# A graph layer on one core: one gather in nine blocks becomes 128 single-row transfers from SyncE

## The chip, the cores and the metric

The kernel runs on one core of a Trainium2 chip. The metric is the device time of one launch in microseconds (us); a version is compared by its median over several launches. [...]

## The reference

8192 nodes with 256 channels, 131072 edges with 64 attributes. `src` is random, `dst` is sorted. All float32.

```python
msg = relu(x[src] + edge_attr @ w_e + b_e)
agg = segment_sum(msg, dst, 8192)
h_local = bn1(relu((x + agg) @ w1 + b1) @ w2 + b2 + x)
# attention inside groups of 32 nodes, 4 heads of 64
q, k, v = split(x @ in_w.T + in_b)
h_attn = bn2(attention(q, k, v) @ out_w.T + out_b + x)
o = h_local + h_attn
o = bn3(o + relu(o @ m_w1 + m_b1) @ m_w2 + m_b2)
return layernorm(x + o)
```

`bn` is a scale and an offset for each channel.

## The kernel before

**Edges.** They are cut into 128 blocks of 1024, in the order of `dst`. A block passes through these steps:

- `gather` (L160): eight indirect DMAs on POOL, each of which fetches 128 rows of 1 KB by an index list into one eighth of the buffer `xs`. There are four `xs` buffers, so block b+4 can be fetched once block b's messages are made. The first 20 blocks fetch from `x`; later ones from `xb`, a copy of `x` in DRAM to which `b_e` has been added.
- `load_edges` (L176): four SP transfers of 128 KB bring the edge attributes into `ea` (two buffers, loaded two blocks ahead of use).
- `edge_transpose` (L193, DVE) turns them, `edge_products` multiplies by `w_e` on PE (L211) into the PSUM bank `pe`, one of two, a bank for each half (pair) of the block. For the first 20 blocks it also puts `b_e` there (L206).
- `edge_messages`: DVE adds `pe` and `xs` (L234, one instruction for each pair), ACT applies relu (L238).
- `edge_hot` (L246) compares indices to make 0/1 matrices; `edge_sums` adds messages by destination on PE (L255, sixteen matmuls a block), ACT copies the result to `ws` (L275); `edge_place` puts it into the right node columns on PE (L290), and DVE adds it to `xT` (L299).

**Nodes.** They are taken in 16 chunks of 512 (eight blocks). `load_nodes` (L306) brings a chunk's 512 KB into `xn` (four buffers) from SP, `attention_front` transposes it on PE (L444, ACT copies it to `xT` at L445) and multiplies by `in_w` (L455), `attention_back` does scores, softmax and the rest, and `dense` runs the two MLPs (matmuls L558), the layer norm, and an SP store of 512 KB from `y` (L616). The last chunk is done by `dense_rows`, 128 nodes at a time: it writes `x` plus the constant row `c3row` into `y` (L630), `sum_of_x` brings that into PSUM as the first term of the output, the layers follow (L641 and on), the norm writes `y` a second time, and SP stores it (L685).

**The copy `xb`.** In the first fourteen blocks or so, `copy_load` (L702) brings 512 KB or 1 MB of `x` into `xp`, `copy_stream` adds `b_e` on DVE (L708) and SP stores it to `xb` (L710). `xp` lies in buffers that `dense` uses later.

**Order.** PE runs in the order of the program text, and until block 26 DVE and ACT do so too; the other engines' instructions, SP's among them, are put in order by a scheduler. The node work is written as generators in four streams, and `work.run(us)` takes steps from them worth that much estimated PE time. A step that yields `REST` sets its stream aside for two calls of `run`:

```python
        if "xn" not in st:
            load_nodes(n0, st, pool)
            yield REST
```

Up to block 104 (`TAIL`) the main loop takes two blocks a turn: gathers for two blocks ahead; products, messages and next loads of the first and of the second block, sums of the turn before; and node work in portions of 0.3, 0.2 and 0.5 of the turn's allowance (0.2, 0.1, 0.2, 0.5 after block 26). After block 104 a planner goes block by block, with estimated due times. `came` is the time at which a block's last gather is expected:

```python
        came = [7.9 + 10.035 * (i + 1) for i in range(NB)]
```

From block 122 (`SPLIT`) on, it takes a block's two pairs one by one. In the very last block the messages are made group by group (256 edges; five additions, the last group in two halves), all issued at one place; then fourteen of the sixteen sums (all but the last gather's), a step of the last `dense_rows`, and the remaining sums.

**What a gather fetches.** Gather t of a block takes edges 128 t to 128 t + 127 of it; within these, edge e lands on partition 32 (e mod 4) + e div 4.

Of the kernel before, what the change touches and what calls it, by code (L numbers as in the profile page):

```python
# [9 lines left out]
FP = mybir.dt.float32  # L10
I32 = mybir.dt.int32
AF = mybir.ActivationFunctionType
ALU = mybir.AluOpType
AX = mybir.AxisListType
PSUM = bass.MemoryType.PSUM
DRAM = bass.MemoryType.DRAM
PE = mybir.EngineType.PE

P = 128
# [4 lines left out]
NB = E // BE  # L24
NH = 4
# [21 lines left out]
LN_EPS = 1e-5  # L47
REST = -1.0
PAUSE = -2.0

# [23 lines left out]
def gnn_kernel(ctx: ExitStack, tc: tile.TileContext, x, src, dst, edge_attr, w, out):  # L74
# [31 lines left out]

    srci = const.tile([P, NB, TB], I32, name="srci")
    rel = const.tile([P, NB, TB], FP, name="rel")
    wrow = const.tile([P, NB], FP, name="wrow")
    width = const.tile([1, 1], I32, name="width")  # L110
# [41 lines left out]

    xs_of = {}

    def gather(b):
        xs = epool.tile([P, NH, TJ, C], FP, name="xs", tag="xs", bufs=4)
        for h in range(NH):
            for j in range(TJ):
                idx = srcd[:, b * NH + h, j : j + 1] if b < ND else srci[:, b, h * TJ + j : h * TJ + j + 1]
                nc.gpsimd.indirect_dma_start(  # L160
                    out=xs[:, h, j, :],
                    out_offset=None,
                    in_=x if b < NX else xb[:, :],
                    in_offset=bass.IndirectOffsetOnAxis(ap=idx, axis=0),
                )
        xs_of[b] = xs
# [48 lines left out]

    def next_edges(b):
        if b < NB:
            edge_transpose(b)
        if b + 2 < NB:
            load_edges(b + 2)  # L220

    def edge_messages(b, pairs=range(0, NH, 2)):

        xs = xs_of[b]
        if b not in msg_of:
            msg_of[b] = epool.tile([P, NH, TJ, C], FP, name="msg", tag="msg", bufs=3)
        msg = msg_of[b]
        n = 2 if b < NB - 1 else 1
        for h in pairs:
            pe = pe_of.pop((b, h))  # L230
            for u in range(0, 2, n):
                hs = slice(h + u, h + u + n)
                for js in [slice(0, TJ)] if n == 2 or h + u < NH - 1 else [slice(j, j + 1) for j in range(TJ)]:
                    nc.vector.tensor_add(  # L234
                        msg[:, hs, js].rearrange("p u i c -> p i u c"), pe[:, js, u : u + n, :],
                        xs[:, hs, js].rearrange("p u i c -> p i u c"),
                    )
                    nc.scalar.activation(msg[:, hs, js], msg[:, hs, js], AF.Relu)  # L238
        between()
# [68 lines left out]
    with tc.tile_pool(name="setup", bufs=1) as sp:  # L308
# [125 lines left out]
    def attention_front(n0, st, pool, bank):  # L434
        if "xn" not in st:
            load_nodes(n0, st, pool)
            yield REST
        xn = st["xn"]
        xT = st["xT"] = pool.tile([P, KC, CH], FP, name="xT", tag="xT", bufs=4)
        hA = st["hA"] = pool.tile([P, KC, CH], FP, name="hA", tag="hA", bufs=4)  # L440
        for k in range(KC):
            ps = bank()
            for t in range(TN):
                nc.tensor.transpose(ps[:, t * P : (t + 1) * P], xn[:, t, k * P : (k + 1) * P], ident)  # L444
            nc.scalar.copy(xT[:, k, :], ps)  # L445
            nc.scalar.activation(
                hA[:, k, :], xT[:, k, :], AF.Identity, scale=s12[:, k : k + 1], bias=cA[:, k : k + 1]
            )
        yield 0.9

        qk = st["qk"] = pool.tile([P, 2 * KC, CH], FP, name="qk", tag="qk")
        for o in range(2 * KC):
            ps = bank()
            for k in range(KC):
                nc.tensor.matmul(  # L455
                    ps, inT[:, k, o * P : (o + 1) * P], xT[:, k, :], start=(k == 0), stop=(k == KC - 1)
                )
# [86 lines left out]

    def dense(n0, st, pool, bank, a=0, z=CH, own=("h1", "m1", "zT", "y", "")):

# [57 lines left out]
        for wt, ts in groups:  # L604
            nc.scalar.activation(rstd[:wt, ts], mv[:wt, ts, 1], AF.Sqrt, bias=eps_t[:wt])
        st["dense"] = z == CH
        yield 0.9 * part
# [6 lines left out]
        for wt, ts in groups:  # L614
            n = wt * (ts.stop - ts.start)
            nc.sync.dma_start(  # L616
                out[ds(n0 + a + ts.start * P, n), :].rearrange("(t p) c -> p t c", p=wt), y[:wt, ts, :]
            )
        yield 0.0

    def dense_rows(n0, st, pool, bank, a, own=("h1", "m1", "zT", "y", ""), ahead=False):
# [82 lines left out]
    def copy_stream(i):  # L704
        for _, c, n in steps[i] if 0 <= i < len(steps) else []:
            xp = xp_of[c]
            for r in range(n * TN):
                nc.vector.tensor_add(xp[:, r, :], xp[:, r, :], be)  # L708
                if r == n * TN - 1:
                    nc.sync.dma_start(rows(xb, c, n), xp)  # L710
                    xp_of.pop(c)
                yield
# [73 lines left out]
    placed = -1  # L786
    with tc.manual_schedule(engines={PE}):

# [8 lines left out]
        for c in range(NCH):  # L797
            st, before, same = chunk[c], chunk[c - 1], chunk[c - 4]
            front = attention_front(c * CH, st, npool, bank)
            if c < 2:  # L800
                next(front)
            work.add(
# [43 lines left out]
        while b < TAIL:  # L846
# [60 lines left out]
        def onward(at):  # L907
            at[:] = [at[0] + 1, 0] if at[1] or at[0] < SPLIT else [at[0], 1]

        while l < NB:  # L910
# [11 lines left out]
            elif p[0] < NB and (p[0] - 1, p[1]) < tuple(m):  # L922
                times[2] = half.get((p[0] - 1, p[1]), added[p[0] - 1])
            if tuple(m) < tuple(p):
                times[3] = came[m[0]]
                if m[0] >= SPLIT and not m[1]:
                    times[3] -= 2.5
            if t >= times[0]:
# [20 lines left out]
            elif t >= times[3]:  # L949

                with ExitStack() as behind:
                    for i, ins in newest.items():
                        if m[0] >= SPLIT or i in ("ws", "xT"):
                            behind.enter_context(tc.issue_after(ins))
                    edge_messages(m[0], (2 * m[1],) if m[0] >= SPLIT else range(0, NH, 2))
                if m[0] < SPLIT:
# [4 lines left out]
            elif t >= times[2]:  # L961
                i, k = p
                if not k and i + 2 < NB:
                    gather(i + 2)
                edge_products(i, (2 * k,) if i >= SPLIT else range(0, NH, 2))
                if k or i < SPLIT:
                    next_edges(i + 2)
                if not k:
                    edge_hot(i)
# [4 lines left out]
        work.finish()  # L974
    fast.close()

# [122 lines left out]
```

## Time and profile before

| | |
|---|---|
| runs | 1317.26, 1316.10, 1314.17 us, median 1316.1 |
| profiled execution: its own time / its span | 1317.09 / 1315.3 us |
| mean granted PE clock in it | 0.968 |
| busy: PE, DVE, POOL, ACT | 91%, 61%, 74%, 45% of the span |
| DMA: bytes, mean rate | 240.34 MB, 183 GB/s |
| chain that ended last: PE, POOL, issue, DVE, DMA | 33%, 32%, 15%, 9%, 7% |
| gathers: 144 from `x`, 864 from `xb` | 969 and 949 ns busy each |
| `ea` loads / `xn` loads / stores of `y` | 512 of 128 KB / 16 of 512 KB / 14 of 512 KB |
| `xp` loads and `xb` stores | 10 of 512 KB and 3 of 1 MB of each |

The span runs from the first to the last instruction; the time of the launch includes what lies around it. Busy shares are averages over stages with different limits: in the first 200 us the DMA engines also carry weights and the copy `xb`. "issue" in the chain is time in which an engine waited for nothing that the profile shows. The first 16 gathers take their indices from a buffer of their own and are listed apart from the 144 and the 864.

### The profile page before, as it was taken

The numbers are of one execution on the slowest core, as the hardware profiler recorded it, in microseconds if no ns is written. First come the engines' busy times: TensorE is split into PE (matmuls) and PEld (weight loads), VectorE is DVE, ScalarE is ACT, GpSimd is POOL, SyncE is SP. The second block draws the span as 40 slices with busy tenths as digits, with TensorE's granted clock in tenths as the row PEclk, the third lists the DMA queues.
The fourth block names the chain that finished last, engine by engine and source line by source line (L and its number), as shares of the span: only waits on it lengthen the run. The fifth ranks groups of instructions, "written<-read, shape, count | busy, mean of one in ns | idle before, by whom it ended". The sixth has DMA issues, their size and how long they took to land.

```text
span 1315.3 us, 21031 instructions
## 1 busy us (share of the span) xinstructions
PE 1200.4 (91%) x7671; PEld 722.5 (55%) x7671; DVE 799.3 (61%) x1630; ACT 587.3 (45%) x842; POOL 977.2 (74%) x1032
## 2 busy tenths in 40 slices
PE   5987989999999989898997998889898999989897
PEld 3544655556555555554554554545555555555665
DVE  6567665756666565745746574565647558475653
ACT  2524343454546263443545444354454445453432
POOL 7777777777777777777777777777777777777772
PEclk8988999999999989998999999989899999999998
DMA  9999876677766666665767666666667567656741
GB/s 241 302 311 271 266 205 174 173 183 195 176 171 173 171 176 164 184 162 154 190 165 184 157 183 169 153 184 171 170 168 191 148 170 190 165 165 159 194 133 50
DMA packets 148921, 240.34 MB, mean 183 GB/s; under 512 B 27950, under 2 KB 112204, under 8 KB 148044
## 3 DMA queue, kind: packets, MB, share of 16 engines
q0 software_dynamic: 49152, 134.28, 38.6%
q1 hardware_dynamic: 98572, 104.65, 29.3%
q8 instruction: 62, 1.02, 0.3%
q14 instruction: 47, 0.39, 0.1%
q10 hardware_dynamic: 1088, 0.00, 0.0%
HBM read 222.06 MB, written 16.78 MB: 182 GB/s over the span
## 4 chain that ended last, share of the span: by engine, by line
PE 33%; POOL 32%; issue 15%; DVE 9%; DMA 7%; ACT 4%; SPq 0%; DVEq 0%; POOLq 0%; ACTq 0%
POOL xs L160 32%; PE at L558 8%; PE pe L211 7%; DMA xs<-xb,srci 4%; PE at L455 4%; PE pw L255 3%; DVE msg L234 3%; PE l L290 2%; PE at L469 2%; PE at L536 2%; PE pe L206 1%; DMA xs<-in_x_dram,srci 1%; DVE bd L516 1%; ACT pr L496 1%; PE at L524 1%
## 5 line engine op out<-in xcount | busy, mean ns | idle before, releaser
L160 POOL DMA_INDIRECT xs<-xb,srci x864 | 820.3, 949 | 263.2 <-issue 251.0
L238 ACT ACTIVATE msg<-msg 128x1024 f32<-128x1024 f32 (+1 forms) x259 | 269.9, 1047 | 407.1 <-DVE msg L234 401.6
L234 DVE TENSOR_TENSOR msg<-pe,xs 128x1024 f32<-128x1024 f32 (+1 forms) x259 | 306.5, 1206 | 203.8 <-PE pe L211 81.1
L211 PE MATMUL pe<-we,eaT 64*128 64x256 f32 x2048 | 268.2, 397 | 16.4 <-ACT pr L496 10.2
L211 PEld LDWEIGHTS pe<-we,eaT 64*128 64x128 f32 x2048 | 192.9, 191 | 121.4 <-issue 63.0
L160 POOL DMA_INDIRECT xs<-in_x_dram,srci x144 | 139.6, 969 | 43.9 <-issue 40.8
L255 PE MATMUL pw<-msg,oh 128*32 128x256 f32 x2048 | 130.0, 383 | 1.1 <-ACT msg L238 0.8
L455 PE MATMUL at<-xT,inT 128*128 128x512 f32 x256 | 121.2, 599 | 3.2 <-ACT xT L445 3.2
L558 PE MATMUL at<-hA,mw 128*128 128x512 f32 (+1 forms) x256 | 116.3, 580 | 2.8 <-DVE hA L568 2.5
L558 PE MATMUL at<-m,mw 128*128 128x512 f32 (+1 forms) x256 | 111.4, 579 | 0.0
L193 DVE STREAM_TRANSPOSE eaT<-ea 128x512 f32<-128x512 f32 x128 | 90.0, 703 | 21.1 <-PE pe L211 19.2
L255 PEld LDWEIGHTS pw<-msg,oh 128*32 128x32 f32 x2048 | 60.0, 109 | 63.3 <-issue 21.4
L290 PEld LDWEIGHTS l<-oh,ws 128*128 128x128 f32 x512 | 72.4, 192 | 26.2 <-issue 20.3
L290 PE MATMUL l<-oh,ws 128*128 128x160 f32 (+4 forms) x512 | 84.2, 304 | 1.7 <-ACT ws L275 1.6
L455 PEld LDWEIGHTS at<-xT,inT 128*128 128x128 f32 x256 | 46.6, 190 | 57.0 <-issue 46.9
L458 ACT ACTIVATE qk<-at,vec 128x512 f32<-128x512 f32 x64 | 43.8, 684 | 70.6 <-PE at L455 70.5
L558 PEld LDWEIGHTS at<-m,mw 128*128 128x128 f32 x256 | 48.1, 193 | 48.4 <-issue 45.4
L558 PEld LDWEIGHTS at<-hA,mw 128*128 128x128 f32 x256 | 46.8, 192 | 50.6 <-issue 41.1
L246 DVE TENSOR_TENSOR oh<-iota_n,rel 128x128 f32<-128x128 f32 x256 | 57.5, 278 | 20.8 <-PE pw L255 20.7
L558 PE MATMUL at<-xT,w 128*128 128x512 f32 (+1 forms) x128 | 61.2, 615 | 6.8 <-DVE xT L299 6.8
L558 PE MATMUL at<-h,w 128*128 128x512 f32 (+1 forms) x128 | 59.8, 590 | 8.2 <-ACT oT L531 6.0
L574 ACT ACTIVATE m<-at,vec 128x512 f32<-128x512 f32 (+1 forms) x64 | 42.1, 658 | 53.8 <-PE at L558 53.7
(153 smaller groups left out, 1250.5 us busy)
## 6 DMA issues: line engine op xcount, KB each, us to landing
ea<-in_edge_attr_dram SPq DMA_DIRECT2D x512, 128.0 KB
xs<-xb,srci POOLq DMA_INDIRECT x864
xn<-in_x_dram SPq DMA_DIRECT2D x16, 512.0 KB
out_dram<-y SPq DMA_DIRECT2D x14, 512.0 KB
xp<-in_x_dram SPq DMA_DIRECT2D x10, 512.0 KB
xb<-xp SPq DMA_DIRECT2D x10, 512.0 KB
xp<-in_x_dram SPq DMA_DIRECT2D x3, 1024.0 KB
xb<-xp SPq DMA_DIRECT2D x3, 1024.0 KB
```

Of the source, the lines that this page charges most:

```text
L160: nc.gpsimd.indirect_dma_start(out=xs[:, h, j, :], out_offset=None, in_=x if b < NX else xb[:, :], in_offset=bass.IndirectOffsetOnAxis(ap= ...
L193: nc.vector.transpose(eaT, ea[:, QR:].rearrange("p (g d) -> p g d", d=ED)[:, :, :QR])
L211: nc.tensor.matmul(pe[:, i, u, :], eaT[rows, h + u], we[rows, :], start=(b >= NX), stop=True, skip_group_check=True)
L234: nc.vector.tensor_add(msg[:, hs, js].rearrange("p u i c -> p i u c"), pe[:, js, u : u + n, :], xs[:, hs, js].rearrange("p u i c -> p i u c"),
L238: nc.scalar.activation(msg[:, hs, js], msg[:, hs, js], AF.Relu)
L246: nc.vector.tensor_tensor(oh[:, ts], iota_n[:, None, :WN].to_broadcast([P, TB // 2, WN]), rel[:, b, ts, None].to_broadcast([P, TB // 2, WN ...
L255: nc.tensor.matmul(pw[h * WN : (h + 1) * WN, i, :], oh_of[b][:, h * TJ + j, :], msg_of[b][:, h, j, :], start=(j == 0), stop=(j == TJ - 1), ...
L290: nc.tensor.matmul(l2[:, k, at : at + wn], ws[:, i, k * P : (k + 1) * P], oh2[:, i, :wn], start=(i == 0 and k == 0), stop=(i == last), ski ...
L455: nc.tensor.matmul(ps, inT[:, k, o * P : (o + 1) * P], xT[:, k, :], start=(k == 0), stop=(k == KC - 1))
L458: nc.scalar.activation(qk[:, o, :], ps, AF.Identity, bias=v_("in_b", o))
L558: nc.tensor.matmul(ps, wt[:, k, o * P : (o + 1) * P], act[:, k, :], start=(k == 0), stop=(k == nk - 1))
L574: newest["relu"] = nc.scalar.activation(m1[:, o, :], layer(mw1, KC, o, hA), AF.Relu, bias=v_("m_b1", o)).ins
```

## The change

In nine blocks, 17, 31, 44, 57, 70, 83, 96, 109 and 122, the eighth gather is left out. Its 128 rows are fetched by 128 transfers of 1 KB that SP starts, each with its address in a register; a `TENSOR_LOAD` on SP fills 16 registers at a time from `srcs`, the clamped indices times 1024. The rows land in `xr` (two buffers). `fetch_rows` spreads them: four rows at each of five places in a turn of two blocks, ten a block in the planner. In such a block the second pair's addition is split in three, the last of which takes `xr` for `xs`.

SP now runs in the order of the text, like PE. So that its transfers are not issued before their data are ready, `put_off` keeps some of them (`ea` loads of the main loop, the `xb` stores, the stores of `y`) for a later `catch_up`. `dense` also asks for the `xn` of the chunk four ahead after it is done with its own. The node work's last portion of 0.5 is cut into 0.3 and 0.2, with rows between: the streams at `REST` see one more `run` a turn.

`dense_rows` writes `x` plus the constant into `xc`, a buffer apart from `y`. The last block's messages are issued group by group, each with a due time. `came` counts the gathers that there are, 1.2544 us each.

```diff
+ROW = 4 * C
+RT = NH * TJ - 1
+ROW_BLOCKS = (17, *range(31, NB, 13))
+RB, RL = 10, 16
...
+    def row_stream():
+        for b in ROW_BLOCKS:
+            while len(xr_of) > 1 or not (b < NX or copied[0]):
+                yield 0
+            xr = xr_of[b] = epool.tile([P, C], FP, name="xr", tag="xr", bufs=2)
+            for e0 in range(0, P, RL):
+                _, rows = nc.values_load_multi_w_load_instructions(
+                    srcs[b : b + 1, e0 : e0 + RL], engines=[SP], min_val=0, max_val=(N - 1) * ROW,
...
+                for i, row in enumerate(rows):
+                    p = (e0 + i) % EQ * QR + (e0 + i) // EQ
+                    nc.sync.dma_start(xr[p : p + 1, :].bitcast(U8), flat[b >= NX][ds(row, ROW)].unsqueeze(0))
...
+                    yield 1
+    row_by_row = row_stream()
+    def fetch_rows(n):
+        for _ in range(n):
+            next(row_by_row, None)
 def gather(b):
...
+                if b in ROW_BLOCKS and h * TJ + j == RT:
+                    continue
...
+    def put_off(turns, do):
+        later.append([turns, do])
+    def catch_up(n=1):
+        for entry in list(later):
+            entry[0] -= n
+            if entry[0] <= 0:
+                later.remove(entry)
+                entry[1]()
...
+    def next_edges(b, turns=0):
         if b < NB:
             edge_transpose(b)
         if b + 2 < NB:
-            load_edges(b + 2)
+            if turns:
+                put_off(turns, lambda: load_edges(b + 2))
+            else:
+                load_edges(b + 2)
...
 def edge_messages(b, pairs=range(0, NH, 2), of_pair=range(2)):
...
+                last = b in ROW_BLOCKS and h + u + n == NH
+                if last:
...
+                    xr = xr_of.pop(b)
+                    nc.vector.tensor_add(msg[:, hs, 0, :], pe[:, 0, u : u + n, :], xs[:, hs, 0, :])
+                    for v in range(u, u + n - 1):
+                        nc.vector.tensor_add(msg[:, h + v, 1, :], pe[:, 1, v, :], xs[:, h + v, 1, :])
+                    nc.vector.tensor_add(msg[:, NH - 1, 1, :], pe[:, 1, u + n - 1, :], xr)
...
+        nc.vector.tensor_scalar(srcs, srci_r[:, RT * P : (RT + 1) * P], 0.0, float(N - 1), ALU.max, ALU.min)
+        nc.vector.tensor_scalar(srcs, srcs, float(ROW), None, ALU.mult)
...
 def dense(n0, st, pool, bank, a=0, z=CH, own=("h1", "m1", "zT", "y", ""), turns=0):
+        catch_up(1000)
...
+        if turns and n0 // CH + 4 < NCH:
...
+            put_off(2, load_ahead)
...
+        if turns:
+            put_off(turns, store)
+        else:
+            store()
...
 def dense_rows(n0, st, pool, bank, a, own=("h1", "m1", "zT", "y", ""), ahead=False):
-        nc.vector.tensor_add(y, st["xn"][:, a // P, :], c3row)
+        xc = pool.tile([P, C], FP, name="xc", tag=own[2])
+        nc.vector.tensor_add(xc, st["xn"][:, a // P, :], c3row)
...
-            nc.tensor.matmul(ps, ident, y, start=True, stop=False, skip_group_check=True)
+            nc.tensor.matmul(ps, ident, xc, start=True, stop=False, skip_group_check=True)
...
-                    nc.sync.dma_start(rows(xb, c, n), xp)
-                    xp_of.pop(c)
+                    put_off(1, lambda c=c, n=n: nc.sync.dma_start(rows(xb, c, n), xp_of.pop(c)))
...
-    with tc.manual_schedule(engines={PE}):
+    with tc.manual_schedule(engines={PE, SP}):
...
-                work.add(DENSE, summed(c), dense(c * CH, st, npool, bank))
+                work.add(DENSE, summed(c), dense(c * CH, st, npool, bank, turns=4))
...
-                next_edges(b + 2)
+                next_edges(b + 2, 1)
+            fetch_rows(2 * RB // 5)
...
-            next_edges(b + 3)
+            next_edges(b + 3, 2 if b else 1)
+            fetch_rows(2 * RB // 5)
...
             work.run((0.3 if stated[0] else 0.1) * per)
+            catch_up()
+            fetch_rows(2 * RB // 5)
             copy_load(b // 2)
+            copied[0] = b > 2 * len(steps)
...
             work.run(0.2 * per)
+            catch_up()
+            fetch_rows(2 * RB // 5)
...
-            work.run(0.5 * per)
+            work.run(0.3 * per)
+            fetch_rows(2 * RB // 5)
+            work.run(0.2 * per)
...
-        came = [7.9 + 10.035 * (i + 1) for i in range(NB)]
+        came = [7.9 + 1.2544 * (TB * (i + 1) - sum(r <= i for r in ROW_BLOCKS)) for i in range(NB)]
...
+                if m[0] == NB - 1:
+                    times[3] -= 2.5 * (NH - 1 - m[1])
+                elif m[0] >= SPLIT and not m[1]:
+                    times[3] -= 5.0
...
+                    if m[0] == NB - 1:
+                        edge_messages(m[0], (m[1] // 2 * 2,), [m[1] % 2])
```

More of the change, by code (lines that the diff above doesn't have):

```diff
@@ L17 @@
 PE = mybir.EngineType.PE
+SP = mybir.EngineType.SP
+ACT = mybir.EngineType.Activation
 P = 128
@@ L150, in bank2 @@
         return pps.tile([P, 2, CH], FP, name="pe", tag="pe", bufs=2)
-    xs_of = {}
+    xs_of, xr_of, xr_full = {}, {}, set()
+    flat = [a.bitcast(U8).rearrange("n c -> (n c)") for a in (x, xb[:, :])]
+    copied = [False]
+    def row_stream():
[6 more added lines that the diff above has]
+                    srcs[b : b + 1, e0 : e0 + RL], engines=[SP], min_val=0, max_val=(N - 1) * ROW,
+                    skip_runtime_bounds_check_because="the indices are clamped to the rows of x when they are kept",
+                )
+                for i, row in enumerate(rows):
+                    p = (e0 + i) % EQ * QR + (e0 + i) // EQ
+                    nc.sync.dma_start(xr[p : p + 1, :].bitcast(U8), flat[b >= NX][ds(row, ROW)].unsqueeze(0))
+                    if e0 + i == P - 1:
+                        xr_full.add(b)
+                    yield 1
[3 more added lines that the diff above has]
+            next(row_by_row, None)
     def gather(b):
@@ L543, in attention_back, with dense @@
             yield 1.7
-    def dense(n0, st, pool, bank, a=0, z=CH, own=("h1", "m1", "zT", "y", "")):
+    def dense(n0, st, pool, bank, a=0, z=CH, own=("h1", "m1", "zT", "y", ""), turns=0):
         assert st["done"]
@@ L606, in dense, with load_ahead @@
         st["dense"] = z == CH
+        if turns and n0 // CH + 4 < NCH:
+            c = n0 // CH + 4
+            def load_ahead():
+                if "xn" not in chunk[c]:
+                    load_nodes(c * CH, chunk[c], pool)
+            put_off(2, load_ahead)
         yield 0.9 * part
@@ L613, in dense, with store @@
             )
[L614 to L618, printed above, removed]
+        def store():
+            for wt, ts in groups:
+                n = wt * (ts.stop - ts.start)
+                nc.sync.dma_start(
+                    out[ds(n0 + a + ts.start * P, n), :].rearrange("(t p) c -> p t c", p=wt), y[:wt, ts, :]
+                )
+        if turns:
+            put_off(turns, store)
+        else:
+            store()
         yield 0.0
@@ L907, in onward @@
         def onward(at):
-            at[:] = [at[0] + 1, 0] if at[1] or at[0] < SPLIT else [at[0], 1]
+            last = 0 if at[0] < SPLIT else NH - 1 if at is m and at[0] == NB - 1 else 1
+            at[:] = [at[0] + 1, 0] if at[1] == last else [at[0], at[1] + 1]
         while l < NB:
```

37 lines of the change are left out of this document (23 added, 14 removed).

## The prediction

> **What bounds the kernel now.** I read the page first: engine times, the forty slices, the costliest groups.
>
> ```profile
> span 1315.3 us, 21031 instructions
> ...
> PE 1200.4 (91%) x7671; PEld 722.5 (55%) x7671; DVE 799.3 (61%) x1630; ACT 587.3 (45%) x842; POOL 977.2 (74%) x1032
> ...
> POOL 7777777777777777777777777777777777777772
> ...
> DMA  9999876677766666665767666666667567656741
> ...
> L160 POOL DMA_INDIRECT xs<-xb,srci x864 | 820.3, 949 | 263.2 <-issue 251.0
> ...
> L160 POOL DMA_INDIRECT xs<-in_x_dram,srci x144 | 139.6, 969 | 43.9 <-issue 40.8
> ```
>
> PE has the largest share, but POOL's row of slices is the telling one: 7 everywhere, never a dip, until the last. Its 26% of idle time is cut evenly between the gathers and belongs to "issue". Two more views say that POOL waits for nobody: its waits, and the gather's own line with its first and last start.
>
> ```profile
> POOL xs L160 <- issue: 298.8, 973, 2.7
> ...
> POOL xs L160 <- DVE msg L234: 2.4, 8, 0.3
> ```
> ```profile
> L160 POOL DMA_INDIRECT xs<-xb,srci x864: 942/946/1087, 209.0 to 1291.2; - x173
> ```
>
> No wait on DVE is longer than the 0.3 us that every gather shows anyway, so no gather waited for its buffer. 864 gathers start between 209.0 and 1291.2: 1082.2/863 = 1.254 us each. The kernel is a row of 1024 gathers at 1.254 us, with a start before it and a tail after it. For it to stay so when POOL gets less to do, PE must have room; the stretches tell:
>
> ```profile
> 60.00:105.00 45.00, 38.65 (x275) 24.36 (x273) 28.58 (x59) 15.10 (x22) 34.34 (x36) 0.92 1.04 314
> 105.00:130.00 25.00, 17.54 (x101) 9.55 (x100) 18.68 (x43) 10.58 (x16) 18.91 (x21) 0.86 0.98 276
> ...
> 350.00:850.00 500.00, 461.75 (x2900) 271.22 (x2896) 295.63 (x577) 227.88 (x310) 378.43 (x400) 0.98 0.66 172
> 850.00:1050.00 200.00, 181.47 (x1108) 108.22 (x1108) 119.17 (x239) 95.69 (x132) 151.57 (x160) 0.92 0.63 171
> 1050.00:1292.00 242.00, 226.13 (x1505) 139.81 (x1504) 151.71 (x317) 106.59 (x167) 183.21 (x194) 1.00 0.63 165
> ```
>
> First number after the stretch is PE's busy time. It idles 38 us of 500, 19 of 200, 16 of 242. The last columns are DMA share and GB/s: full before 130 us, two thirds later.
>
> **The gathers removed.** In blocks 17, 31, 44 ... 122 the eighth gather goes: nine blocks, 9 x 1.254 = 11.3 us off POOL. In the changed order of instructions POOL has 16 + 143 + 856 = 1015 gathers. All of it lies on the path as long as no gather starts to wait. PE must then do the same work in 1.25 us less per thirteen blocks (about 130 us); its idle time by the rows above is 8 to 12 us per 130. So I count the full 11.3.
>
> A rule speaks against this. The Trainium skill, "DMA: Bandwidth & Descriptors", section "Issuing engines are not separate DMA queues": transfers started by different engines share the same 16 engines, and spreading the starts only saves the sequencer's starting time, "which is usually small relative to the DMA itself". By it moving rows to SyncE gives about nothing. The trace differs here: with the DMA share at 0.66 the starting time itself, 1.254 us, is the limit.
>
> **What SyncE gets.** 9 x 128 = 1152 one-row transfers, and a register load per 16 rows.
>
> ```profile
> L176 SPq DMA_DIRECT2D ea<-in_edge_attr_dram x512: 311/432/1795, 3.2 to 1251.9; - x171
> ```
> ```profile
> L326 SPq DMA_DIRECT2D vec_r<-in_L_gnn_bn_g_dram x3: 231/233/268, 11.2 to 16.1; - x3
> ```
> ```profile
> L978 SPq TENSOR_LOAD <-width x1: 533/533/533, 1312.0 to 1312.0; - x1
> ```
> ```profile
> 0.75 2.05 DMA srcd<-in_src_dram
> ...
> 9.71 5.54 DMA dsti_r<-in_dst_dram
> ...
> 16.76 5.34 DMA in_r<-in_L_gnn_in_w_dram
> ```
>
> No one-row transfer with its address in a register is in this trace. From below it costs SyncE 0.233 us (vec_r), from above 0.432 (ea); I take 0.35. Ten rows a block: 3.5 us, the register load 0.5, four ea loads 1.7: about 6 of the 10 us that a block takes. In the changed order every transfer waits for the eighth before it, so landing times count too: 2.05 us for a small one on a quiet queue, 5.3 to 5.5 for half a megabyte and more in a busy one. Fourteen transfers per block at a mean of 3 us are 14 x 3 / 8 = 5.3 us. Later than 200 us SyncE thus keeps up, and the rows cost nothing; their cover is that slack of some 4 us per block.
>
> **Before 200 us it is not covered.** SyncE is now kept in program order, and the DMA engines are full. From the first load of block 2 to the last of block 17 the changed queue holds 223 transfers, 128 of them rows; before it held 93.
>
> ```profile
> 49.37 1.75 SPq L176 DMA_DIRECT2D ea<-in_edge_attr_dram  x4
> ...
> 84.68 0.38 SPq L306 DMA_DIRECT2D xn<-in_x_dram  x1
> ...
> 105.84 0.34 SPq L710 DMA_DIRECT2D xb<-xp  x1
> ```
> ```profile
> 104.01 1.15 PE L290 MATMUL l<-oh,ws 128*128 128x112 f32 x8
> 105.08 1.13 PE L206 MATMUL pe<-be,sel 64*128 64x512 f32 x4
> 106.05 1.03 PE L211 MATMUL pe<-we,eaT 64*128 64x256 f32 x8
> ...
> 121.97 1.09 PE L444 MATMUL at<-ident,xn 128*128 128x128 f32 x8
> 124.94 1.13 PE L455 MATMUL at<-xT,inT 128*128 128x512 f32 x2 [1.87 <-ACT xT L445]
> 126.25 4.56 PE L455 MATMUL at<-xT,inT 128*128 128x512 f32 x10 [0.19 <-ACT xT L445]
> ```
> ```profile
> 67.94 0.70 DVE L193 STREAM_TRANSPOSE eaT<-ea 128x512 f32<-128x512 f32 x1
> ...
> 114.79 2.35 DVE L234 TENSOR_TENSOR msg<-pe,xs 128x1024 f32<-128x1024 f32 x2
> ...
> 186.00 1.23 DVE L234 TENSOR_TENSOR msg<-pe,xs 128x1024 f32<-128x1024 f32 x1 [0.50 <-PE pe L211]
> ```
> ```profile
> 127.18 0.95 POOL L160 DMA_INDIRECT xs<-in_x_dram,srci  x1 [0.30 <-DVE xp L708]
> ...
> 188.84 0.94 POOL L160 DMA_INDIRECT xs<-in_x_dram,srci  x1 [0.30 <-DVE oh L279]
> ```
>
> One wait stands out. Chunk 2's node load went out at 84.68 and its transposes ran at 121.97. Splitting the last stretch of attention work in two makes a rest of two turns shorter, so PE reaches these transposes right after the placement that stood at 104.01, ahead of block 8's products. Their load now follows, on SyncE, the store that left at 105.84, four rows and two loads. It leaves at about 109; with 2.5 MB in front and itself, at 314 GB/s, it lands 8 us later, some 117 (from below: 109 + 5.3 = 114; from above 124, with the rows' own landings in the chain). PE stands still from about 105 to 117; queued behind are block 8's products, and DVE waits for those. Transposes 1.1, the wait for ACT 1.9, eight matmuls 3.6 (4.56 for ten), a first pair of products 1.1 + 1.0: first message at 125.5, second 1.7 later and 1.2 long, done by 128.5 to 130 instead of 117.1. The gather of block 12, which takes block 8's buffer, wants to start at 127.2. So POOL waits 2 to 3 us. Against that, PE's 7.5 idle us in 105 to 130 are used up by the same wait, and the tightest later buffer (block 14's messages end at 187.2, the gather starts at 188.84: 1.6 us) gains what POOL has already lost. I count +3.0 us, ends 0 (landing at 114) and 8 (landing at 124).
>
> **The tail.**
>
> ```profile
> 1287.44 1.91 DMA out_dram<-y
> ...
> 1293.39 2.07 PE at L641 x10
> ...
> 1296.41 2.44 PE pw L255 x14
> ...
> 1299.48 0.55 PE pw L255 x2
> ...
> 1300.66 0.53 PE l L290 x4
> ```
> ```profile
> 1293.68 2.54 DVE L234 TENSOR_TENSOR msg<-pe,xs 128x512 f32<-128x512 f32 x5
> ```
>
> The chain goes through a store: y is its source, and the sum of x and the constant waited for it until 1289.4. With its own buffer that wait is gone; next late is the xT sum behind it, which also needs the placement before it, so of the store's 1.9 us I let the L641 layers gain 0.8, an estimate; they then end at 1295.6 instead of 1296.4. The last block's five additions ran in one piece from 1293.68; taken by groups, the first two or three lie before it, and only the last two hang on the last gather. The fourteen sums, 2.44 us because they waited for messages, shrink to about 1.0. 0.8 + 1.4 = 2.2 off, ends 0 (PE's layers hold the sums as before) and 4. What follows the sums is the same work.
>
> **The rest at nothing.** Splitting an addition: the five pieces cost 2.54, the same columns in two whole ones 2.35; DVE is 61% busy. Stores put off feed nothing on the path before the tail. The index arithmetic is two DVE instructions in the setup.
>
> **Sum.** The profiled execution took 1317.1, 1.8 more than its span and 1.0 more than the median, 1316.1. 1317.1 - 11.3 + 3.0 - 2.2 = 1306.6; against the median 1305.6.
>
> **Rivals.**
> The early wait costs POOL nothing and the tail gives all: 1317.1 - 11.3 - 1.0 = 1304.8 less 2.2 to 4.0; about 1302. For it: DVE's and PE's idle time there. 0.20.
>
> PE becomes the bound: its idle stretches are waits for DVE and ACT that don't shrink, and half of the 11.3 is lost: 1305.6 + 5.6 = 1311. Against it: PE's clock in 850 to 1050 was 0.92 and the gathers still never waited. 0.12.
>
> Transfers bound, as the rule of the Trainium skill has it: the 11.3 comes back as landing time. 1317.1 + 3.0 - 2.2 - 1.0 = 1316.9. Against: shares of 0.63 to 0.66. 0.05.
>
> Slower: SyncE's chain falls behind before 200 us. 223 transfers in the 150 us until block 17's loads are 0.67 us each, eight in flight: break-even at a mean landing of 5.4 us. Each us above makes the queue 223/8 = 28 us late at its end. Loads lead their use by 67.9 - 49.4 - 5.3 = 13 us, the buffer margin gives 1.6; beyond these POOL stands still, and xb, needed from 209.0, comes late too. From 6.4 us on, this eats the whole gain (13.5 + 14.6 = 28); at 6.7 it is 36 - 14.6 = 22 lost: 1317.1 - 13.5 + 22 - 1.0 = 1325. For it: 5.3 to 5.5 in the rows above. Against it: more than half of the transfers are single rows. 0.13.
>
> That the change does not do what it says is ruled out by the 1015 gathers.
>
> **Numbers.** The forecast has 0.50 and its own span, 1302.5 to 1310.5. About 0.2%, 2.6 us, is what a measurement of this kernel can tell from no change. Faster: 0.50 + 0.20 + 0.12, less 0.03 for a PE-bound end nearer to 1316, 0.79; same: that 0.03 and the rule's rival, 0.08; slower: 0.13. The range reaches from 1300.8 (1317.1 - 11.3 - 4.0 - 1.0, no early wait) to 1316.5; the rule's rival and the slow one, 0.18, lie above.
>
> **What would show it.** After: 1015 gathers at 1.254 us with one or two waits of POOL for msg between 120 and 200 us and none later, the last gather starting at about 1283 (1291.2 - 11.3 + 3); PE waiting for a DMA ahead of chunk 2's transposes; 21 us instead of 23 from the last gather's end to the span's. I am wrong if POOL's slices dip anywhere after 200 us, if a row takes SyncE over 0.6 us, or if ea's transposes wait for loads.

## The result and the profile after

The changed kernel takes 1387.35 us (median of 4 runs, 1383.02 to 1389.22); the kernel before 1315.73. The ratio is 1.0543, 95% interval 1.0528 to 1.0557: slower by 72 us, where 10 us less was forecast, and far above the range. On some chips the kernel before itself takes about 2000 to 2040 us, at a granted clock of 0.82; runs that fell there are told apart, at the end of the experiments, and nothing is drawn from them.

The page of the changed kernel, cut to the lines that answer to those of before (PE is TensorE, DVE VectorE, ACT ScalarE, POOL GpSimd, SP SyncE):

```profile
span 1385.9 us, 23312 instructions
...
PE 1201.7 (87%) x7671; PEld 724.4 (52%) x7671; DVE 801.0 (58%) x1650; ACT 592.4 (43%) x842; POOL 969.2 (70%) x1023
...
PE   5982979999696989989798989989698994999887
...
POOL 7774667777677777777777777777667777467760
...
PE 54%; DMA 14%; DVE 10%; POOL 9%; issue 7%; ACT 3%; SPq 2%; DVEq 0%; POOLq 0%; ACTq 0%
```

PE's work is the same to 1.3 us (1200.4 before), POOL's is 8 us less. But POOL's row now dips, early (slices 4 to 6) and in three later places, and the chain has turned over: POOL fell from 32% to 9%, PE rose from 33% to 54%. What POOL and PE waited for (us in total, times, longest):

```profile
POOL xs L195 <- DVE msg L293: 51.7, 16, 15.1
POOL xs L195 <- DVE msg L289: 14.0, 1, 14.0
```
```profile
PE at L506 <- DMA xn<-in_x_dram: 76.8, 9, 26.6
PE at L586 <- DVE bd L578: 23.2, 6, 6.6
```

L506 is the transposes at the head of a chunk (the line numbers are each kernel's own). Nine times PE stands there until the node load `xn` has landed, 76.8 us in all; in the kernel before that wait does not appear. While PE stands, no products are made, so no messages, so no `xs` buffer comes free, and POOL waits too. So the span is about 8 us until PE's first matmul, PE's work and PE's idle time after that. The work is the same 7671 matmuls in every kernel, but its measured time differs by up to 12 us from run to run, so differences of "sum" are differences of time only together with "work". In the table the idle time is cut by the work done: the cuts are the first product (edge attributes times `w_e`) of blocks 8, 28, 104 and 122; each number is the sum of the gaps between PE's matmuls in us (a gap that ends at a cut counts behind it; the last column takes in some 5.5 us after the last matmul), worked out from the trace of one profiled execution, while "time" is the median of the runs. Where the kernel is the same up to a cut the numbers differ by up to 2 us (before, e9, e13 and e14 up to block 8). The other rows of the table are experiments told below (rows: single-row transfers; pin: DVE's transpositions held in place).

```
                          to 8   8-28  28-104 104-122  122-end   sum    work    time
before                    13.0   12.8    59.4    10.5     11.3  106.9  1200.4  1315.7
after                     37.4   13.0    85.5    28.3     11.7  176.0  1201.7  1387.4
e6  after, no rows        26.1   12.8    53.1    21.1     10.1  123.1  1192.8  1326.1
e10 after, SyncE free     36.7   13.1    76.8    28.1     11.7  166.3  1198.5  1375.3
e7  after + pin           34.1   13.1    60.3    28.4     11.7  147.5  1194.6  1353.1
e8  ... rows from 31 on   25.5   14.2    61.1    28.5     11.7  141.1  1189.6  1341.7
e11 ... xn earlier        15.0   13.4    60.5    30.3     11.7  130.9  1190.4  1331.8
e15 ... pin to the end    13.0   14.3    60.5    26.3      9.1  123.3  1195.1  1328.2
e16 ... all nine blocks   20.0   24.0    60.7    26.3      9.1  140.2  1196.3  1345.1
e12 no rows, xn earlier   14.0   16.0    56.3    19.7     10.1  116.1  1189.6  1317.5
e9  before, 9 gathers out 12.7   12.8    52.1    12.5     10.8  100.9  1201.2  1311.5
e14 before, 27 out        13.3   12.8    46.2     9.9     11.6   93.9  1191.4  1295.1
e13 before, tail's edits  14.6   12.8    57.7    10.8     11.6  107.5  1196.1  1314.2
```

After minus before is 69.1 us of idle time, against 70.6 us of span. It was lost in three places: 24 us up to block 8, 26 us in blocks 28 to 104, 18 us in blocks 104 to 122.

**The early place.** PE, SyncE and the wait in the changed kernel (start, duration, and in brackets the idle time before it and what ended that):

```profile
101.50 1.84 PE L349 MATMUL l<-oh,ws 128*128 128x112 f32 x8
129.90 1.97 PE L506 MATMUL at<-ident,xn 128*128 128x128 f32 x8 [26.56 <-DMA xn<-in_x_dram]
```
```profile
92.34 11.63 SPq L177 DMA_DIRECT2D xr<-in_x_dram  x8
104.02 0.92 SPq L936 DMA_DIRECT2D mw<-in_L_gnn_m_w_dram  x2
105.04 5.17 SPq L177 DMA_DIRECT2D xr<-in_x_dram  x8
110.31 1.77 SPq L211 DMA_DIRECT2D ea<-in_edge_attr_dram  x4
112.17 0.38 SPq L789 DMA_DIRECT2D xb<-xp  x1
112.65 2.69 SPq L177 DMA_DIRECT2D xr<-in_x_dram  x4
115.40 0.85 SPq L781 DMA_DIRECT2D xp<-in_x_dram  x2
116.30 0.49 SPq L365 DMA_DIRECT2D xn<-in_x_dram  x1
```

It is the wait that the prediction named, at the instruction that it named. But the load left at 116.3, not at 109, and PE went on at 129.9, not at 117. Sixteen rows took SyncE 16.8 us here: each transfer waits for the eighth before it, and the DMA share was 0.94 and 0.90 in the two stretches.

**Later.** A piece from the middle: SyncE, DVE and PE around chunk 5.

```profile
336.30 1.76 SPq L211 DMA_DIRECT2D ea<-in_edge_attr_dram  x4
338.17 5.30 SPq L177 DMA_DIRECT2D xr<-xb  x12
356.50 1.77 SPq L211 DMA_DIRECT2D ea<-in_edge_attr_dram  x4
359.64 1.30 SPq L177 DMA_DIRECT2D xr<-xb  x4
361.04 0.41 SPq L365 DMA_DIRECT2D xn<-in_x_dram  x1
```
```profile
347.49 1.20 DVE L293 TENSOR_TENSOR msg<-pe,xs 128x1024 f32<-128x1024 f32 x1
...
350.50 1.38 DVE L682 TENSOR_SCALAR y<-y,mv,rstd 128x256 f32<-128x256 f32 x4
351.79 2.84 DVE L578 STREAM_TRANSPOSE bd<-pr 32x512 f32<-32x512 f32 x4
354.67 0.62 DVE L358 TENSOR_TENSOR xT<-l,xT 128x448 f32<-128x448 f32 x1
355.21 0.65 DVE L338 TENSOR_SCALAR oh<-iota_n,wrow 128x160 f32<-128x160 f32 x2
355.78 1.28 DVE L228 STREAM_TRANSPOSE eaT<-ea 128x512 f32<-128x512 f32 x2
```
```profile
354.78 3.68 PE L586 MATMUL at<-bd,vn 128*64 128x128 f32 x32 [4.99 <-DVE bd L578]
366.07 1.94 PE L506 MATMUL at<-ident,xn 128*128 128x128 f32 x8 [7.61 <-DMA xn<-in_x_dram]
```

SyncE issues nothing from 343.5 to 356.5: it stands (12.9 us of it) at an edge load whose buffer is freed by a transposition of edge attributes (L228). The twelve rows before it had cost only 5.3 us. The transposition is late because DVE does layer norm, softmax and `xT` first; two of them come in one go at 355.78, with no idle time before. The node load stands behind that edge load, leaves at 361.0, and PE waits 7.6 us. The same place in the kernel before, on DVE:

```profile
333.36 1.23 DVE L234 TENSOR_TENSOR msg<-pe,xs 128x1024 f32<-128x1024 f32 x1
334.50 0.70 DVE L193 STREAM_TRANSPOSE eaT<-ea 128x512 f32<-128x512 f32 x1
```

There the transposition comes right behind the second message addition. In the order of DVE's instructions that is so for 75 of the 78 transpositions of blocks 26 to 103; in the changed kernel for only 28 of them, and the others have up to 32 other instructions in between. The text that orders them is the same: from block 26 on it is the scheduler that orders DVE.

### The profile page after: what moved, and what is told of

Its sections match the earlier page's. It is cut to its first block, busy times and chain, and to the rows that moved or that the text cites. A ratio compares the mean times of both kernels' runs of the same rounds, so it can differ in the third digit from the quotient of the medians.

```text
span 1385.9 us, 23312 instructions
## 1 busy us (share of the span) xinstructions
PE 1201.7 (87%) x7671; PEld 724.4 (52%) x7671; DVE 801.0 (58%) x1650; ACT 592.4 (43%) x842; POOL 969.2 (70%) x1023
## 4 chain that ended last, share of the span: by engine, by line
PE 54%; DMA 14%; DVE 10%; POOL 9%; issue 7%; ACT 3%; SPq 2%; DVEq 0%; POOLq 0%; ACTq 0%
PE at L620 15%; PE pe L246 11%; POOL xs L195 9%; PE at L517 6%; PE pw L314 5%; DMA xs<-xb,srci 4%; PE at L598 4%; DMA xn<-in_x_dram 4%; PE l L349 3%; DMA ea<-in_edge_attr_dram 3%; DVE msg L293 3%; PE at L531 2%; PE pe L241 1%; PE at L586 1%; DMA xb<-xp 1%
## 5 line engine op out<-in xcount | busy, mean ns | idle before, releaser
L293 DVE TENSOR_TENSOR msg<-pe,xs 128x1024 f32<-128x1024 f32 (+1 forms) x250 | 294.1, 1204 | 172.8 <-PE pe L246 87.4
L228 DVE STREAM_TRANSPOSE eaT<-ea 128x512 f32<-128x512 f32 x128 | 89.4, 702 | 14.9 <-PE pe L246 7.1
L506 PE MATMUL at<-ident,xn 128*128 128x128 f32 x128 | 22.5, 335 | 78.0 <-DMA xn<-in_x_dram 76.8
L305 DVE TENSOR_TENSOR oh<-iota_n,rel 128x128 f32<-128x128 f32 x256 | 59.4, 283 | 26.5 <-PE pw L314 26.1
L630 DVE SCALAR_TENSOR_TENSOR hA<-at,s,hA 128x512 f32<-128x512 f32 (+1 forms) x32 | 22.8, 713 | 84.9 <-PE at L620 84.8
```

The lines of the kernel that those rows point to most:

```text
L228: nc.vector.transpose(eaT, ea[:, QR:].rearrange("p (g d) -> p g d", d=ED)[:, :, :QR])
L293: nc.vector.tensor_add(msg[:, hs, js].rearrange("p u i c -> p i u c"), pe[:, js, u : u + n, :], xs[:, hs, js].rearrange("p u i c -> p i u c"),
L305: nc.vector.tensor_tensor(oh[:, ts], iota_n[:, None, :WN].to_broadcast([P, TB // 2, WN]), rel[:, b, ts, None].to_broadcast([P, TB // 2, WN ...
```

## The experiments

The first theory was *order*: SyncE in the order of the text holds the node loads behind edge loads. Its rival was *rows*: the 1152 transfers. When the first of these runs had come back, a third took their place, *transposes*: with rows on SyncE the scheduler moves DVE's transpositions back, and SyncE, in order, passes the delay on to the node loads.

**No rows (e6).** `ROW_BLOCKS = ()`, so that all 1024 gathers are back.

> The changed kernel without a single row transfer: all 1024 gathers back on POOL, everything else as changed, SyncE in the order of the text too. Theory 'order' (a chunk's node load stands in SyncE's queue behind edge loads that wait for DVE's transposes, and PE waits for it): most of the loss stays, 1360 to 1385, and PE still waits for xn ahead of the chunks' transposes. Rival 'rows' (the 1152 small transfers themselves slow SyncE and the DMA queues): about 1316 to 1325.

1326.1 us in one run, beside 1316.6 of the kernel before: 1 us above the rival's range, and 61 of the 72 us are gone. Of *order* one wait is left:

```profile
PE at L506 <- DMA xn<-in_x_dram: 18.3, 1, 18.3
```

It is chunk 2's. SyncE still stands at edge loads (625 us in all), and nobody minds: in this kernel, as before, 75 of the 78 transpositions stand right behind the messages, and the later node loads leave 6 to 19 us ahead of their use. So the change without its rows costs 10 us in this one run; POOL's waits in it, 9.4 us beyond its usual step, all lie before 200 us. The table shows one thing more: of the 18 us of idle time that the changed kernel adds in blocks 104 to 122, 10.6 are there without any row. That the rows do the rest does not say how.

**Transpositions pinned (e7), no early rows (e8), nine gathers out (e9), SyncE free (e10).** e7 binds DVE's order alone (SyncE and PE keep theirs; of ACT's 842 instructions, which the scheduler also orders, 810 stand in the same order as in the changed kernel):

```diff
+        held.close()
-        nc.vector.transpose(eaT, ...)
+        ins = nc.vector.transpose(eaT, ...).ins
+        if NV + 2 <= b < TAIL + 2:
+            held.enter_context(tc.issue_after(ins))
```

> The changed kernel with all rows; only DVE's order is altered: from block 28 to block 105 whatever the text has behind a transposition of edge attributes is issued behind it on DVE, so that the transposition comes right behind the messages as it does in the kernel before (in the changed kernel it stands up to 33 DVE instructions later). Theory 'transposes' (the rows make the scheduler put these transpositions late on DVE, SyncE stands in front of the edge load that waits for them, and node loads behind it leave too late): 1324 + 2 - 11 + 15 for the early stage = 1330, between 1320 and 1340. Rival 'rows' (1152 transfers take SyncE's time and the queues'): 1370 to 1390.

1353.1 us, ratio 1.0285 (1.0253 to 1.0317): 34 us of the 72, above what *transposes* had allowed and well below what *rows* had. In the table the stage that was pinned, blocks 28 to 104, goes from 85.5 to 60.3 us of idle time; before it was 59.4. With 1024 rows still fetched, that stage loses nothing more against the kernel before. It gains nothing either: with the same gathers left out and no rows (e9) it idles 52.1 us, and in e7 the softmax's transposed weights `bd` are what PE waits for there (36.8 us, 5.2 before). Of the 34 us, 25 are idle time of this stage and 3 idle time before block 8; the other 7 are PE's work, which took less time in this stage (697.7 and 690.2 us, at granted clocks of 0.948 and 0.968); whether the order has to do with that is not shown. Of PE's nine waits for `xn` two are left:

```profile
PE at L511 <- DMA xn<-in_x_dram: 38.6, 2, 23.5
```

e8 is e7 with `ROW_BLOCKS = tuple(range(31, NB, 13))`.

> As e7, and block 17 keeps its eighth gather, so that no row is fetched before 200 us (eight blocks left). If the early loss above that of the kernel without rows (POOL's waits until 205 us add up to 25.6 us in the changed kernel, to 10.6 us without rows) comes from the rows of block 17: 15 less than e7 and a gather more, about 1316. If SyncE's order alone makes it: as e7, 1331.

1341.7 us, 1.0187 (1.0156 to 1.0218): 11.4 us less than e7, 8.6 of them up to block 8. The rows of block 17 cost that much, near the 14 us that were expected of them (15, less a gather). The total of 1316 that was expected fell: it was counted from e7's forecast of 1330, and the loss of blocks 104 to 122 is still there.

e9 is the kernel before with `continue` at the eighth gather of the nine blocks, `be` in place of the fetched rows (with the addition split in three as in the change), and `came` counting the gathers that there are.

> The kernel before, with the nine gathers left out and nothing in their place (the last addition of those blocks takes the row of b_e instead of fetched rows, so the values are not the reference's); SyncE, the stores and the tail are as before. If the gathers are the path, as the first term of the sum had it: 1316 - 11.3, 1304 to 1307. If PE holds the end instead: 1313 to 1317.

1311.5 us, 0.9960 (0.9941 to 0.9978): neither. POOL's rows:

```profile
span 1310.5 us, 21037 instructions
...
L164 POOL DMA_INDIRECT xs<-xb,srci x856: 942/946/1467, 208.1 to 1280.6; - x172
```

The last gather starts at 1280.6 instead of 1291.2, the 11.3 us less that the sum promised, to 0.7. But 30.0 us follow it instead of 24.1: 5.9 are given back. PE had its work still to do. This run settles one rival as well: with the additions split and no rows, 75 of the 78 transpositions still stand right behind the messages, so the split additions by themselves do not move them.

e10 is the changed kernel with `manual_schedule(engines={PE})`.

> The changed kernel with rows, SyncE's instructions ordered by the scheduler (only PE in the order of the text); DVE's transpositions stay as late as in the changed kernel. If SyncE's fixed order is needed for the loss: node loads pass the edge loads, 1305 to 1325. If the late transpositions are enough by themselves: 1340 to 1370. Rival 'rows': 1370 to 1390.

1375.3 us, 1.0458 (1.0429 to 1.0488): freeing SyncE gives back 12 us only, and the time lies in the range of *rows*, above what the late transpositions by themselves were given. DVE's order in it is, but for a few places, that of the changed kernel, and PE waits 65.8 us for `xn`, seven times. The theory that SyncE's order must be fixed for the loss falls here. But the scheduler, free to choose, kept 1736 of SyncE's 1753 transfers in the order of the changed kernel, and most node loads still stand right behind edge loads and rows. So the run does not show that the late transpositions are enough under any order: late transpositions with the node loads ahead of the edge loads were not measured on such a chip.

**Node loads earlier (e11, e12), the tail alone (e13), 27 gathers out (e14).**

```diff
-            put_off(2, load_ahead)
+            load_ahead()
...
+            if b in (4, 6):
+                load_nodes((b // 2) * CH, chunk[b // 2], npool)
```

> As e8 (transpositions pinned on DVE, no rows before 200 us), and the node loads leave earlier: those of chunks 2 and 3 stand in SyncE's text at blocks 4 and 6, and each dense step asks for the next chunk's load at once, not two turns later. What is left of the loss in e8 by PE's idle time up to block 8 (25.5 us against 13.0 before) and in blocks 104 to 113 (20.4 against 3.5) are waits for xn. Theory 'node loads': both go, 1341.7 - 12 - 15 = 1315, between 1309 and 1320. If they are something else that only ends at the same instructions (the rows' share of SyncE, the planner's due times): 1333 to 1342.

1331.8 us, 1.0123 (1.0107 to 1.0138): 9.9 us less, where 27 were expected, and just outside both ranges. Up to block 8 PE's idle time falls from 25.5 to 15.0 us. The first line of the edit moved six of the later loads four transfers forward in SyncE's order; the others, chunk 15's among them, stand where they stood, and chunk 15's is still late:

```profile
PE at L511 <- DMA xn<-in_x_dram: 16.1, 1, 16.1
```

> As e6 (no rows at all), with the node loads earlier as in e11. Theory 'node loads': the 13 us of PE's waiting before block 8 go, 1326 - 10 to 13 = 1313 to 1317. If SyncE's fixed order costs by itself: 1322 to 1327.

1317.5 us, 1.0012 (0.9996 to 1.0029). Without rows the two early loads undo the early loss (26.1 to 14.0 us of idle time), and nothing that can be measured is left in the time. By the table that is a balance: PE idles 9 us longer than before, all of it in blocks 104 to 122, and its work took 11 us less in the profiled execution.

e13 has from the change only `xc` and the last block's messages, with their due times, in the kernel before.

> The kernel before with the tail's edits alone: x plus the constant in a buffer of its own, the last block's messages group by group with due times of their own. The prediction's term was 2.2 us less, 0 to 4: 1312 to 1316. If PE's work holds the tail anyway: 1315.5 to 1317.

1314.2 us, 0.9995 (0.9986 to 1.0004): not told from no change. In the profiled execution the last gather is followed by 22.3 us instead of 24.1. PE's idle time in blocks 104 to 122 is 10.8 us, so the tail's edits are not what spoils that stage.

e14 is e9 with `ROW_BLOCKS = tuple(range(20, NB, 4))`.

> The kernel before with the eighth gather left out of 27 blocks (20, 24, ... 124; the row of b_e is added instead, so the values are not the reference's): POOL gets 33.9 us less to do. If PE holds the end once POOL is relieved, as the 30.0 us after the last gather in e9 say: no better than e9, 1306 to 1312. If e9's loss was only in its tail: 1316 - 34 + 6 = 1288 to 1292.

1295.1 us, 0.9840 (0.9821 to 0.9858), between the two again. POOL is done 35.2 us earlier (last gather at 1256.0), the end comes 20.9 earlier. So in these two runs POOL's time was worth 0.4 and 0.6 of itself at the end: it takes idle time from PE (blocks 28 to 104: 59.4, 52.1, 46.2 us with 0, 9 and 27 gathers out), and PE does not give as much as POOL saves.

**Pinned to the end (e15, e16).** The condition becomes `if NV + 2 <= b:`; e16 has all nine row blocks.

> As e11 (rows in eight blocks from 31 on, node loads earlier), with DVE's transpositions pinned in the planner's blocks too, up to the end. What is left of the loss in e11 is PE's 16.1 us of waiting for the node load of chunk 15, which stands on SyncE behind an edge load that waits for the transposition of block 109. Theory 'transposes': that wait goes, 1331.8 - 16 = 1316, and if the gathers' half gain (e9: 4.5) shows too, 1311; so 1309 to 1318. If the rows' transfers themselves delay that load: 1328 to 1333.

1328.2 us, 1.0091 (1.0067 to 1.0115): a number in the rival's range, though not by the rival's cause. The mechanism held and the gain did not: the 16.1 us of waiting for chunk 15's load are gone, but PE's idle time in blocks 104 to 122 falls by 4 us only. Other waits have come up there, the softmax's transposed weights (`bd`) first, 13.1 us in two pieces:

```profile
PE at L591 <- DVE bd L583: 13.1, 2, 6.9
```

42.3 us follow the last gather, and all gathers together waited 3.9 us, in three waits after 1180 us. Between e15 and the kernel before 12 us stay unexplained in detail; the table says where they lie (26.3 against 10.5 us), and e12, without rows, has half of that.

> As e15 with all nine row blocks of the change, 17 among them. Theory 'transposes': the rows' own cost is what block 17's 128 transfers do before 200 us. By e7 against e8 11.4 us dearer than e15; with the node loads of chunks 2 and 3 gone ahead of them, part of it: 1315 to 1325. If block 17's rows only hurt through chunk 2's node load: 1 us below e15.

1345.1 us, 1.0212 (1.0187 to 1.0238), 17 us above e15 and above both expectations. PE's idle time says where: 7 us up to block 8 and 10 in blocks 8 to 28. With node loads out of their way, block 17's rows hurt in another place. What DVE and SyncE waited for between 60 and 200 us, in e16:

```profile
DVE xp L792 <- DMA xp<-in_x_dram: 27.3, 3, 11.1
```
```profile
SPq L177 <- DMA xp<-in_x_dram: 20.3, 9, 3.5
```

A row waits on SyncE until an earlier copy load of 512 KB or 1 MB has landed, the next copy load stands behind the rows, and DVE, in the order of the text until block 26, stands at the copy's addition with messages behind it. In e15 the first wait is 4.6 us. This chain is read from the waits; no run took it away by itself.

**Runs elsewhere.** On chips on which the kernel before took 2008 to 2027 us, e1 (the kernel of e9) gave a ratio of 0.9994, e2 (that of e6) 1.0105, e4 (that of e10) 1.0336; e3, the changed kernel with the node loads of chunks 2 to 15 started by ACT, 1.0394, and in one more run (e5) 2106 us beside 2008. The changed kernel itself was not run there. In e1 POOL waited 635 us for messages: gathers are no limit there, and none of it tests the theories above. The last two runs fell there as well: e17, which is e11 with rows only in blocks 31 to 96 (1.0333), and e18, the same with SyncE free (1.0328).

> The changed kernel with rows, but the node loads of chunks 2 to 15 are started by ACT instead of SyncE; nothing else. Theory 'order': PE's 76.8 us of waiting for xn go, 1305 to 1325. Rival 'rows': the rows are all still there, 1370 to 1390.

> As e11 (node loads earlier, transpositions pinned from block 28 to 105), with rows in the six blocks 31 to 96 only, so that no row is fetched while the planner orders the work after block 104. If the rows are what spoils that last part (PE's idle time in blocks 104 to 122 is 30 us in e11, 26 in e15, 20 without rows, 10.5 before): e12's 1317.5 less half of 6 x 1.254 us = 1313 to 1317. If the pinning or the earlier loads spoil it: 1324 to 1332.

> As e17, with SyncE's instructions ordered by the scheduler. If SyncE's order in the text costs the remaining 9 us in blocks 104 to 122 that e12 has beyond the kernel before: 1306 to 1312, better than the kernel before. If not: 1313 to 1318.

So three questions stay open: what ACT as the issuer of the node loads would give, what spoils blocks 104 to 122 (about half of it is there without rows), and whether any version with rows beats the kernel before. None that was measured beside the 1316 us did.

## Why the prediction was wrong, point by point

**The gathers (-11.3).** POOL's part was right, the end's part was not. The step that failed is "So I count the full 11.3", from PE's idle 8 to 12 us per 130. Idle time was there, but what PE waited for was not looked at. In the 500 us from 350 to 850, where the forecast counted 38 idle us, its waits add up to 36.6 us, and every one of them ended on DVE or ACT; the two longest:

```profile
PE pe L486 <- DVE msg L234: 9.8, 5, 2.8
PE at L593 <- DVE zT L586: 6.3, 4, 2.8
```

Messages wait for gathers in their turn, so a part of this shrinks with fewer gathers: e9 took 6.0 us from PE's idle time, and measured 4.5 at the end. That is the rival "PE becomes the bound", priced at half, with a chance of 0.12. The rule of the Trainium skill ("DMA: Bandwidth & Descriptors", section "Issuing engines are not separate DMA queues") that moving starts between engines saves little was set aside because starting time is the limit here. e14 bears that out in the main: 33.9 us less of starting gave 20.9 at the end. The rule's rival had the loss come from landing times; e7's 34 us came back with every transfer from block 28 on still in place.

**Before 200 us (+3.0, ends 0 to 8).** Right wait, wrong size: PE stood 26.6 us, and POOL's waits up to 211 us were 14.8, 3.9 and 5.8 us beyond its usual step. The term that was mis-sized is the load's departure and landing. The queue ahead of it was counted at SyncE's cost per issue and a drain of 8 us, but it moved at the pace of landings: sixteen rows took 16.8 us, and the load 13.6 from its issue at 116.3 to PE's start at 129.9. The slower rival had this chain, with blocks' edge loads late and 1325 us; what came late were a node load (e8 to e11: 9.9 us) and, behind it, the copy's loads (e16).

**After 200 us (0).** This is the step that decided the sign: "Later than 200 us SyncE thus keeps up, and the rows cost nothing". The price of a row was not the fault (0.35 us; the trace has 0.228 each, and twelve in 5.3 us with what lies between them, 0.44 each), though the load of 16 registers took 1.25 us (median of 72), not 0.5. SyncE did keep up: it still stood 277 us at edge loads, waiting for transpositions. What was not looked at is that an engine whose order a scheduler makes can be reordered by work that is added on another engine. DVE got no work worth naming (1650 instructions instead of 1630) and lost its order, and 25 of the 69 us of idle time went there, as e7 shows, whose time is 34 us less. The count of DVE's instructions between a message and the next transposition could have been taken before any run. Why the scheduler moved them was not tried; that it reckons edge loads behind rows to land later is a guess.

**Blocks 104 to 122 (not seen).** 18 us, of which e6 and e12 have about half without rows. In the changed kernel PE waited 15.0 us for chunk 15's node load; with that gone (e15), other waits filled most of the room. The cause stays open.

**The tail (-2.2).** 1.8 us in e13's median, but its interval takes in zero. In the changed kernel PE's work, not the last gather, sets the tail: 42.9 us follow it.

**What would show it.** The forecast had named dips of POOL after 200 us as proof against it. There are three: slice 11, 29 and 30, 35 and 36 of its row (346 to 381, 970 to 1040 and 1178 to 1247 us). The last gather started at 1343.0, not at about 1283. The other two signs did not show: a row took SyncE 0.228 us, and transpositions waited 5.2 us for edge loads in all, 1.7 before.

## What to carry to other kernels

A change that adds transfers to one queue can move the instructions of an engine to which it gives next to nothing, where a scheduler sets the order (here 28 of 78 transpositions kept their place, 75 before): compare the order of every engine, not only of those that the diff names, and look for instructions that free the buffers of the queue. SyncE, in order, passed the wait of one edge load on to all behind it (12.9 us at 343.5), so what must not be late (here 512 KB for the next chunk) should not stand behind a load that waits for another engine. And before the full price is put on an engine's saved time, sum the idle time of the next busiest engine and ask what it waits for: its waits for other engines are not won with it (here 4.5 of 11.3 us reached the end).

## What was not expected of the hardware

A one-row transfer with its address in a register costs SyncE 0.228 us of issue, no more than a small one with a fixed address (0.233). With eight transfers in flight the same row took from 0.44 us (twelve in 5.3, at a DMA share of 0.79) to 1.45 us (eight in 11.6, at 0.94) of the queue's time. And the gathers kept their pace in every kernel in which they did not wait, whatever SyncE and DVE did: 1.254 us in e9 (from 208.1 to 1280.6, 855 steps), 1.253 in e12, 1.254 in e14.
